# A fused graph layer and attention layer: several loads and vector instructions placed anew, and the last group of batches in another order

## The chip, the cores and the metric

The kernel runs on one core of a Trainium2 chip. The metric is the time on the device, in microseconds (us), from the first to the last instruction of the program and the little that lies around it; it is given as the median of several runs. The core has four compute engines with queues of their own: PE (TensorE, matrix products), DVE (VectorE), ACT (ScalarE) and POOL (GpSimd). SP (SyncE) only issues DMAs. Each engine works through its own list of instructions in order, and semaphores make an instruction wait for those of other engines that it depends on.

## The reference

The input is x of 64 batches of 256 rows of 512 numbers, and a symmetric 256 x 256 adjacency matrix of zeros and ones. Two layers follow each other, each with a residual and a norm:

```python
def _L0_gnn_ref(x, adj, W, b):
    Wi, Wj = (W[:, :Din], W[:, Din:])
    mi = einsum('bkd,od->bko', x, Wi)
    mj = einsum('bkd,od->bko', x, Wj)
    a = adj.astype(x.dtype)
    deg = a.sum(axis=1)
    return deg[None, :, None] * (mi + b) + einsum('ij,bjo->bio', a, mj)

def _L1_gnn_ref(h, adj, Wq, bq, Wk, bk, Wv, bv, Wo, bo):
    q, k, v = (split_heads(h @ W.T + c) for W, c in ((Wq, bq), (Wk, bk), (Wv, bv)))
    scores = einsum('bhqd,bhkd->bhqk', q, k) / 8
    scores = where(adj == 0, -inf, scores)
    out = einsum('bhqk,bhkd->bhqd', softmax(scores), v)
    return out.transpose(0, 2, 1, 3).reshape(b, n, 512) @ Wo.T + bo

x = _layernorm(x + _L0_gnn_ref(x, adj, L0_gnn_W, L0_gnn_b))
x = _layernorm(x + _L1_gnn_ref(x, adj, L1_gnn_Wq, ..., L1_gnn_bo))
```

There are 8 heads of 64 numbers. All is float32.

## The kernel before

**Groups and stages.** Batches are worked in 32 groups of two. The loop over g from 0 to 30 does the attention of group g and, woven into it, the graph layer (`Layer0`, objects `first` and `second`) of the two batches of group g + 1, called b1 and b2; b3 is the first batch of group g + 2. At the end of an iteration the v, q and k projections of group g + 1 are made. The last group, g = 31, has an end of its own after the loop. All groups are written out, with no loop on the chip.

**Products.** A product of float32 matrices is made from three products of rounded parts: each operand is cut into head, low and diff. `split_head` runs on ACT, `split_diff` on DVE, `split_low` on DVE or POOL as its last argument says. In PSUM one bank (`px`, or half of `pxy`) takes head times head and low times lift, another (`py`) takes diff times diff. The weights' parts (`factor`, 768 KB each) are read again from DRAM for each group into a ring of seven tiles: `bring` issues the load of the next one when one has been used up.

**PSUM banks.** There are three sorts: three single banks (`bank`), two tiles of two banks for scores (`score_banks`), and one for attention values (`value_bank`). The letter of a projection's step says from where its two banks come: "M" two single ones, "S" one pair of score banks, "A" one single one and the value bank.

**Attention.** Eight head pairs of a group, numbered w, each give: `scores(g, w)` (PE), of which the returned function adds the mask (DVE L910), takes the exponential (ACT L914) and adds the two halves of the keys (POOL L924); `values(g, w)` (PE); and after each second pair `divide_two`, which copies the values (ACT L958), forms the denominators on PE, takes their reciprocal (DVE L1009), moves it across partitions by two DMAs, and puts up a product for POOL that `multiply()` does (L952). The result, `aoT`, is cut into parts (`ao_parts`: batch i, chunks 0 and 1 are `upper`, 2 and 3 are `lower`; the head goes to a tile tagged qT, the diff to one tagged kT, the low part to one tagged v) and multiplied with the output weights in `o_steps`: `begin`, `go_on` and `own` for batch 0 of the group, `others` for batch 1. `adds(n)` (L830, L833) adds the product of row block n to the residual.

**The graph layer's result** of a row block goes through `add` (L613, neighbours' sum), `stat` (DVE L496 to L502, POOL L504) and `give` (ACT L509, L510), is sent to DRAM by `send_h`, fetched in another layout by `fetch_h`, and turned on DVE by `turn_h` (L517); then it is cut into the parts hA, hL and hD for the projections. x itself comes in twice: by `load_x` in rows (tile xh, of which there are five) and by `load_xB` for turning (`turn_x`); `x_head`, `x_low` and `x_diff` cut the turned x.

**Order.** Nearly every instruction goes through `in_order`, so each engine keeps the order in which the program calls it. Calls that follow each other in the program but belong to different engines have no order between them, apart from their dependencies. In the text, h11 and h10 are the row blocks 1 and 0 of b1; diff(upper), low(upper) and the like are the parts of `ao_parts(g, 1, ...)`, batch 1 of the group, unless batch 0 is named.

**The end.** `project(i, t, chunks)` multiplies `aoT` of row block t of batch i with the output weights in full float32, `finish` adds it, norms and stores. Before, the loop ran over the pairs w from 0 to 7, with the scores two pairs ahead:

```python
    last = NB * NC - 1
    for w in range(last + 1):
        values(g, w)
        multiply()
        if w == last - 1:
            project(0, 0, (0, 1, 2, 3))
            finish(0, 0)
        elif w % 2 and w < last:
            divide_two(g, w)
        if w + 2 <= last:
            scores(g, w + 2)()
```

Of the kernel before, what the change touches and what calls it, by code (L numbers as in the profile page):

```python
# [219 lines left out]
def unshifted_path(ctx, tc, flag, x, adj, wiT, wjT, b0, wqT, bq, wkT, bk, wvT, bv, woT, bo, out):  # L220
# [73 lines left out]
    def load_x(b):  # L294
        if b < B:
            xh[b] = p5.tile([P, NT, D], F32, tag="xh", name="xh")
            in_order(nc.sync.dma_start(out=xh[b], in_=x[b].rearrange("(t p) d -> p t d", p=P)))
# [738 lines left out]
    def projection_steps(g, kinds="", paired=True):  # L1036
        if paired:
            v = [v_pair(g, 0, "MS", False), v_pair(g, 1, "AS", True)]
        else:
            v = [v_step(g, i, t, kinds[NT * i + t], (i, t) == (NB - 1, 0)) for i in range(NB) for t in range(NT)]  # L1040
        q, k = ([qk_step(g, store, tag, bias, m, kinds[m]) for m in range(NC)]
                for store, tag, bias, kinds in ((qT, "qT", bq_sb, "SSSM"), (kT, "kT", bk_sb, "MMMA")))
        return v, q, k

    warm = value_bank("warm")
# [86 lines left out]
    for g in range(NG - 1):  # L1132
# [37 lines left out]
        if g:  # L1170
            for _ in range(NC):
                coming.pop(0)
                bring()

        values(g, 2)
        values(g, 3)
# [25 lines left out]

        values(g, 4)
        values(g, 5)
        load_x(b3)
        multiply()
        if g == 0:
            add_output_bias(0)
# [3 lines left out]
        now, later = scores(g, 6), scores(g, 7)  # L1212
        aoP[g] = three(("qT", "kT"))
        aoP[g].insert(1, None)
        now()
        split_head(*ao_parts(g, 0, lower))
        begin, go_on, own, adds, others = o_steps(g, early[0], lambda t: turn_h(b2, t))
        begin()
        later()
        second.neighbours()  # L1220
        values(g, 6)
        invert()
        fetch_h(b1, 1)
        values(g, 7)
        split_diff(*ao_parts(g, 0, lower))
        second.add(0)
        aoP[g][1], = three(("v",))
        first.give(0)
        multiply()
        second.add(1)  # L1230
        send_h(b1, 0)
        total_up = divide_two(g, 7)
        split_head(*ao_parts(g, 1, upper))
        fetch_h(b1, 0)
        go_on()
        split_low(*ao_parts(g, 0, lower), nc.gpsimd)
        own()
        h11 = turn_h(b1, 1)
        split_head(*h11)
        second.stat(1)  # L1240
        second.give(1)
        split_low(*ao_parts(g, 1, upper), nc.vector)
        split_diff(*ao_parts(g, 1, upper))
        multiply()
        split_head(*ao_parts(g, 1, lower))
        second.stat(0)
        adds(0)
        split_low(*ao_parts(g, 1, lower), nc.gpsimd)
        second.give(0)
        split_diff(*ao_parts(g, 1, lower))  # L1250
        h10 = turn_h(b1, 0)
        send_h(b2, 1)
        send_h(b2, 0)
        split_diff(*h11)
        split_head(*h10)
        adds(1)
        split_low(*h10, nc.vector)
        split_diff(*h10)
        total_up()
        fetch_h(b2, 1)  # L1260
        fetch_h(b2, 0)
        split_low(*h11, nc.gpsimd)
        first, second = Layer0(b3) if b3 < B else None, Layer0(b3 + 1)
        v, q_, k = projection_steps(g + 1)
        end = finish_steps(g)
        others()
        turn_x(b3)
        if g == 0:
            make_first("wj", 0)
            make_first("wj", 1)  # L1270
        v[0]()
        if g == 0:
            make_first("wj", 2)
            make_first("wj", 3)
            end_makes()
        x_head(b3)
        x_low(b3)
        v[1]()
        x_diff(b3)
        load_xB(b3 + 1)  # L1280
        run([end[0], q_[0], end[1], k[0], end[2], q_[1]])
        if first:
            first.graph_half(1, (0, 2, 1))
            first.take(1)
        run([end[3], k[1], end[4]])
        add_output_bias(b1)
        if g + 2 < NG:
            add_bias(b3)
        run([q_[2]])
        load_x(b3 + 1)  # L1290
        add_output_bias(b2)
        if first:
            first.cut_up(1)
        run([k[2], q_[3], end[5]])
        turn_x(b3 + 1)
        run([scores(g + 1, 0), scores(g + 1, 1)])
        if g + 2 == NG:
            k[3]()

    g = NG - 1
    wo_sb = p1.tile([P, NC, D], F32, tag="hA", name="wo_sb")
    load_wo(wo_sb, 0)
    outs = {}

    def project(i, t, chunks):
        if chunks[0] == 0:
            outs[i, t] = bank("po")
        for c in chunks:  # L1310
            matmul(outs[i, t], aoT[g][:, c, i * N + t * P:i * N + (t + 1) * P], wo_sb[:, c, :],
                   start=(c == 0), stop=(c == NC - 1))

    def finish(i, t):
# [4 lines left out]
        nc.sync.dma_start(out=out[b].rearrange("(t p) d -> p t d", p=P)[:, t, :], in_=r)  # L1319

    last = NB * NC - 1
    for w in range(last + 1):
        values(g, w)
        multiply()
        if w == last - 1:
            project(0, 0, (0, 1, 2, 3))
            finish(0, 0)
        elif w % 2 and w < last:
            divide_two(g, w)
        if w + 2 <= last:  # L1330
            scores(g, w + 2)()
    inverses = divide_at_once(g, last)
    project(0, 1, (0, 1, 2, 3))
    finish(0, 1)
    project(1, 0, (0, 1))
    project(1, 1, (0, 1))
    end_values(inverses)
    for t in range(NT):
        project(1, t, (2, 3))
        finish(1, t)  # L1340


# [49 lines left out]
```

## Time and profile before

| | us |
|---|---|
| median of 3 runs | 2952.39 (2951.73 to 2953.07) |
| the profiled execution | 2951.97 |
| its span, first to last instruction | 2950.1 |
| PE busy in the span | 2878.1 |
| DVE busy | 2265.1 |
| POOL busy | 1482.3 |
| ACT busy | 1309.4 |
| from one group's start to the next, steady groups | 90.1 to 91.6 |

The profile is of one execution. PE was granted 0.999 of its clock over the span. Times in views of the timeline are counted from the span's first instruction. In the table of waits, a line says which engine waited at which tile for whom, the total, how often, and the longest. In the timeline a line gives start, duration, engine, line of the kernel, operation, tiles (out<-in), and in brackets the idle time of the engine just before with what ended it. All matrix products stand at L286, since a helper issues them, so they are told apart by their tiles.

### The profile page before, as it was taken

To read this page: it belongs to the slowest core of one execution; us is meant where nothing else is said; L and a number is where in the kernel's file an instruction comes from. 1 tells how busy PE (TensorE), PEld (TensorE's weight loads), DVE (VectorE), ACT (ScalarE), POOL (GpSimd) and SP (SyncE) were. 2 spreads that over 40 slices of the span, in tenths; PEclk is the share of its full clock that TensorE was granted. 3 is DMA by queue.
4 is the path that set the end of the run, shared out by engine and by line. 5 is a ranking of instruction groups with operands and counts; after the bars stand their busy time and mean duration, and the time that the engine had idled before them with its cause. 6 is when DMAs were issued, how large, how long until landed. Compare 5 with 4: busy or idle time off the path is not lost.

```text
span 2950.1 us, 45509 instructions
## 1 busy us (share of the span) xinstructions
PE 2878.1 (98%) x16902; PEld 2140.1 (73%) x16902; DVE 2265.1 (77%) x3275; ACT 1309.4 (44%) x2412; POOL 1482.3 (50%) x1049
## 2 busy tenths in 40 slices
PE   9999999999999999999999999999999999999998
PEld 6577777777777777777777777777777777777775
DVE  5777787777877778877778777787777787777875
ACT  4444444444444444444444444444444444444443
POOL 3555555454555455454545544555545555454553
PEclk9999999999999999999999999999999999999999
DMA  7577766777666776667776677766677766777653
GB/s 251 194 258 239 247 218 218 255 245 266 217 219 239 266 247 230 212 226 264 242 247 222 221 249 252 268 212 215 238 267 240 246 214 215 257 248 261 213 211 116
DMA packets 303345, 690.54 MB, mean 234 GB/s; under 512 B 25744, under 2 KB 171280, under 8 KB 302864
## 3 DMA queue, kind: packets, MB, share of 16 engines
q1 hardware_dynamic: 282784, 588.02, 58.4%
q10 hardware_dynamic: 20336, 99.56, 9.5%
q8 instruction: 136, 2.23, 0.3%
q14 instruction: 89, 0.73, 0.1%
HBM read 589.04 MB, written 81.79 MB: 227 GB/s over the span
## 4 chain that ended last, share of the span: by engine, by line
PE 77%; DVE 15%; POOL 3%; DMA 3%; issue 1%; SPq 1%; ACT 1%; POOLq 0%; DVEq 0%; ACTq 0%
PE px L286 26%; PE pxy L286 20%; PE py L286 13%; PE ps L286 7%; PE pav L286 5%; PE pa L286 3%; DVE hF L517 2%; DMA hB<-h_cols 2%; DVE kT L683 2%; DVE spread L1009 2%; DVE st L496 2%; PE po L286 2%; DVE xh L833 1%; PE den L286 1%; DVE xh L830 1%
## 5 line engine op out<-in xcount | busy, mean ns | idle before, releaser
L924 POOL TENSOR_TENSOR pk<-pe 128x512 f32<-128x512 f32 x256 | 347.4, 1368 | 729.5 <-ACT pe L914 729.5
L914 ACT ACTIVATE pe<-pe 128x1024 f32<-128x1024 f32 x256 | 271.0, 1059 | 176.9 <-DVE pe L910 176.9
L504 POOL TENSOR_TENSOR rstd<-ve,mhalf 128x1 f32<-128x1 f32 x256 | 167.5, 654 | 343.4 <-DVE below L502 313.2
L910 DVE TENSOR_TENSOR pe<-ps,maskT 128x1024 f32<-128x1024 f32 x256 | 297.2, 1200 | 3.6 <-PE ps L286 3.6
L1009 DVE RECIPROCAL spread<-den 128x256 f32<-128x256 f32 x127 | 222.7, 1754 | 81.7 <-ACT aoT L958 51.8
L686 POOL TENSOR_TENSOR hL<-hF,hA 128x512 fp32r<-128x512 f32 x93 | 166.4, 1789 | 229.1 <-ACT hA L680 229.1
L774 DVE TENSOR_TENSOR kT<-py,kT 128x512 f32<-128x512 f32 x128 | 88.5, 692 | 226.2 <-ACT kT L773 226.2
L286 PE MATMUL ps<-qT,kT 64*128 64x256 f32 x2048 | 256.6, 390 | 0.0
L286 PE MATMUL pav<-pe,v_sb 128*32 128x256 f32 x4096 | 248.4, 382 | 3.5 <-DVE kT L774 1.5
L286 PEld LDWEIGHTS ps<-qT,kT 64*128 64x128 f32 x2048 | 187.3, 187 | 68.6 <-PE pav L286 26.3
L510 ACT ACTIVATE xh<-xh,shift,rstd 128x512 f32<-128x512 f32 x256 | 208.8, 816 | 8.6
L286 PEld LDWEIGHTS pav<-pe,v_sb 128*32 128x32 f32 x4096 | 120.0, 110 | 116.8 <-issue 24.4
L680 ACT ACTIVATE hA<-hF 128x512 fp32r<-128x512 f32 x124 | 78.3, 632 | 278.5 <-DVE hF L517 255.5
L286 PE MATMUL px<-factor,x_head 128*128 128x512 f32 x720 | 200.2, 400 | 0.0
L286 PE MATMUL py<-factor,x_diff 128*128 128x512 f32 x720 | 192.8, 390 | 2.0 <-ACT kT L773 2.0
L368 POOL TENSOR_TENSOR xh<-xh,degb 128x1024 f32<-128x1024 f32 x64 | 182.5, 2853 | 22.8 <-ACT degb L365 20.9
L286 PE MATMUL px<-factor,x_low 128*128 128x512 f32 x720 | 192.8, 390 | 0.0
L952 POOL TENSOR_TENSOR aoT<-aoT,spread 128x512 f32<-128x512 f32 x127 | 165.9, 1306 | 41.6 <-DMA spread<-spread 35.4
L686 POOL TENSOR_TENSOR x_low<-xT,x_head 128x1024 fp32r<-128x1024 f32 x60 | 144.2, 2403 | 67.6 <-ACT x_head L680 64.7
L286 PE MATMUL py<-hD,factor 128*128 128x512 f32 x640 | 175.9, 397 | 2.2 <-ACT kT L773 2.2
L286 PE MATMUL px<-hA,factor 128*128 128x512 f32 x640 | 175.7, 397 | 0.0
L496 DVE BATCH_NORM_STATS2 st<-xh 128x6 f32<-128x512 f32 x256 | 174.3, 681 | 0.2
(160 smaller groups left out, 6809.1 us busy)
## 6 DMA issues: line engine op xcount, KB each, us to landing
factor<-wi SPq DMA_DIRECT2D x120, 768.0 KB, 8.7
factor<-wo SPq DMA_DIRECT2D x120, 768.0 KB, 6.2
factor<-wv SPq DMA_DIRECT2D x93, 768.0 KB, 7.8
factor<-wk SPq DMA_DIRECT2D x93, 768.0 KB, 7.0
factor<-wq ACTq DMA_DIRECT2D x62, 768.0 KB, 7.6
factor<-wq SPq DMA_DIRECT2D x62, 768.0 KB, 7.4
xB<-in_x_dram SPq DMA_DIRECT2D x256, 128.0 KB, 4.1
xh<-in_x_dram SPq DMA_DIRECT2D x64, 512.0 KB, 3.9
```

What stands on the lines that cost most here:

```text
L286: in_order(nc.tensor.matmul(*args, **kw))
L368: in_order(nc.gpsimd.tensor_tensor(xh[b], xh[b], degb, ALU.add))
L496: order(nc.vector.bn_stats(st, t))
L504: order(nc.gpsimd.tensor_tensor(rstd, ve, mhalf, ALU.pow))
L510: order(nc.scalar.activation(t, t, AF.Identity, bias=shift, scale=rstd))
L686: in_order(engine.tensor_tensor(parts[1], src, parts[0].bitcast(F32), ALU.subtract))
L774: in_order(nc.vector.tensor_add(dst, Y, dst))
L910: in_order(nc.vector.tensor_add(pe.rearrange("p j t q -> p j (t q)"), ps.rearrange("p j t q -> p j (t q)"), maskT.rearrange("p t q -> p (t ...
L914: in_order(nc.scalar.activation(flat, flat, AF.Exp, scale=QSCALE, accum_out=etot[:, NB * g + i, pr:pr + 1]))
L924: in_order(nc.gpsimd.tensor_tensor(pk, pe[:, :, 0, :], pe[:, :, 1, :], ALU.add))
L952: in_order(nc.gpsimd.tensor_tensor(d, d, spread, ALU.mult))
L1009: in_order(nc.vector.reciprocal(rden, den))
```

## The change

It touches no formula and no tile of the steady loop; it moves calls, and rewrites the end.

- In the loop: `load_x(b3)` is called before pair 2's values, not after pair 5's. In the stretch from pair 6's scores to `others()`, the calls of ACT, DVE and POOL work are in another order, and `split_low` of h10 is POOL's, where it was DVE's. `load_xB(b3 + 1)` and `x_diff(b3)` come before `v[1]()`, where they came after. The finishing steps `end[...]`, the output biases and `load_x(b3 + 1)` stand elsewhere among the q and k projections.
- The last group: its projections q2, k2, q3 and k3 are no longer made in the iteration before but between the head pairs of the last group. The pairs go in the order 0, 1, 4, 5, 2, 3, 6, 7, so that the first four need only q0, k0, q1 and k1. `project` makes half of the chunks at a time, and three of these halves come between the pairs too. The output weights lie in two tiles of other tags. For this group, the banks of q2 and k3 are single ones ("SSMM", "MMMM").

```diff
--- before.py
+++ after.py
@@ -1039,7 +1039,9 @@
         else:
             v = [v_step(g, i, t, kinds[NT * i + t], (i, t) == (NB - 1, 0)) for i in range(NB) for t in range(NT)]
         q, k = ([qk_step(g, store, tag, bias, m, kinds[m]) for m in range(NC)]
-                for store, tag, bias, kinds in ((qT, "qT", bq_sb, "SSSM"), (kT, "kT", bk_sb, "MMMA")))
+                for store, tag, bias, kinds in (
+                    (qT, "qT", bq_sb, "SSSM" if g < NG - 1 else "SSMM"),
+                    (kT, "kT", bk_sb, "MMMA" if g < NG - 1 else "MMMM")))
         return v, q, k
 
     warm = value_bank("warm")
@@ -1171,6 +1173,7 @@
             for _ in range(NC):
                 coming.pop(0)
                 bring()
+        load_x(b3)
 
         values(g, 2)
         values(g, 3)
@@ -1202,7 +1205,6 @@
 
         values(g, 4)
         values(g, 5)
-        load_x(b3)
         multiply()
         if g == 0:
             add_output_bias(0)
@@ -1212,103 +1214,114 @@
         now, later = scores(g, 6), scores(g, 7)
         aoP[g] = three(("qT", "kT"))
         aoP[g].insert(1, None)
+        split_head(*ao_parts(g, 0, lower))
         now()
-        split_head(*ao_parts(g, 0, lower))
         begin, go_on, own, adds, others = o_steps(g, early[0], lambda t: turn_h(b2, t))
         begin()
         later()
         second.neighbours()
         values(g, 6)
         invert()
+        second.add(1)
+        first.give(0)
+        values(g, 7)
+        aoP[g][1], = three(("v",))
         fetch_h(b1, 1)
-        values(g, 7)
+        second.add(0)
+        send_h(b1, 0)
+        multiply()
         split_diff(*ao_parts(g, 0, lower))
-        second.add(0)
-        aoP[g][1], = three(("v",))
-        first.give(0)
-        multiply()
-        second.add(1)
-        send_h(b1, 0)
         total_up = divide_two(g, 7)
-        split_head(*ao_parts(g, 1, upper))
-        fetch_h(b1, 0)
         go_on()
         split_low(*ao_parts(g, 0, lower), nc.gpsimd)
         own()
         h11 = turn_h(b1, 1)
+        second.stat(1)
+        split_head(*ao_parts(g, 1, upper))
         split_head(*h11)
-        second.stat(1)
         second.give(1)
+        multiply()
         split_low(*ao_parts(g, 1, upper), nc.vector)
-        split_diff(*ao_parts(g, 1, upper))
-        multiply()
+        fetch_h(b1, 0)
         split_head(*ao_parts(g, 1, lower))
         second.stat(0)
+        split_diff(*ao_parts(g, 1, upper))
+        split_low(*ao_parts(g, 1, lower), nc.gpsimd)
         adds(0)
-        split_low(*ao_parts(g, 1, lower), nc.gpsimd)
         second.give(0)
         split_diff(*ao_parts(g, 1, lower))
+        send_h(b2, 1)
         h10 = turn_h(b1, 0)
-        send_h(b2, 1)
-        send_h(b2, 0)
         split_diff(*h11)
         split_head(*h10)
+        total_up()
         adds(1)
-        split_low(*h10, nc.vector)
         split_diff(*h10)
-        total_up()
+        send_h(b2, 0)
         fetch_h(b2, 1)
-        fetch_h(b2, 0)
         split_low(*h11, nc.gpsimd)
+        split_low(*h10, nc.gpsimd)
         first, second = Layer0(b3) if b3 < B else None, Layer0(b3 + 1)
         v, q_, k = projection_steps(g + 1)
-        end = finish_steps(g)
+        fetch_h(b2, 0)
         others()
         turn_x(b3)
         if g == 0:
             make_first("wj", 0)
             make_first("wj", 1)
         v[0]()
+        load_xB(b3 + 1)
         if g == 0:
             make_first("wj", 2)
             make_first("wj", 3)
             end_makes()
         x_head(b3)
+        x_diff(b3)
+        v[1]()
         x_low(b3)
-        v[1]()
-        x_diff(b3)
-        load_xB(b3 + 1)
-        run([end[0], q_[0], end[1], k[0], end[2], q_[1]])
+        end = finish_steps(g)
+        end[0]()
+        q_[0]()
+        end[1]()
+        k[0]()
+        q_[1]()
+        end[2]()
         if first:
             first.graph_half(1, (0, 2, 1))
             first.take(1)
-        run([end[3], k[1], end[4]])
-        add_output_bias(b1)
+        k[1]()
+        end[3]()
+        end[4]()
+        if g + 2 < NG:
+            q_[2]()
         if g + 2 < NG:
             add_bias(b3)
-        run([q_[2]])
+        if g + 2 < NG:
+            k[2]()
+        add_output_bias(b1)
         load_x(b3 + 1)
-        add_output_bias(b2)
         if first:
             first.cut_up(1)
-        run([k[2], q_[3], end[5]])
+        if g + 2 < NG:
+            q_[3]()
+        end[5]()
         turn_x(b3 + 1)
+        add_output_bias(b2)
         run([scores(g + 1, 0), scores(g + 1, 1)])
-        if g + 2 == NG:
-            k[3]()
 
 
 
     g = NG - 1
-    wo_sb = p1.tile([P, NC, D], F32, tag="hA", name="wo_sb")
-    load_wo(wo_sb, 0)
+    wo_sb = [p1.tile([P, 2, D], F32, tag=t, name="wo_sb") for t in ("xlow", "xdiff")]
+    for n, t in enumerate(wo_sb):
+        load_wo(t, 2 * n)
     outs = {}
 
-    def project(i, t, chunks):
-        if chunks[0] == 0:
-            outs[i, t] = bank("po")
-        for c in chunks:
-            matmul(outs[i, t], aoT[g][:, c, i * N + t * P:i * N + (t + 1) * P], wo_sb[:, c, :],
+    def project(i, t, half):
+        if half == 0:
+            outs[i, t] = score_bank("po") if i and t else bank("po")
+        for c in range(2 * half, 2 * half + 2):
+            matmul(outs[i, t], aoT[g][:, c, i * N + t * P:i * N + (t + 1) * P], wo_sb[half][:, c % 2, :],
                    start=(c == 0), stop=(c == NC - 1))
 
     def finish(i, t):
@@ -1319,24 +1332,31 @@
         nc.sync.dma_start(out=out[b].rearrange("(t p) d -> p t d", p=P)[:, t, :], in_=r)
 
     last = NB * NC - 1
-    for w in range(last + 1):
+    turns = (0, 1, 4, 5, 2, 3, 6, 7)
+    remaining = [q_[2], k[2], q_[3], k[3]]
+    for n, w in enumerate(turns):
+        if n < len(remaining):
+            remaining[n]()
         values(g, w)
         multiply()
-        if w == last - 1:
-            project(0, 0, (0, 1, 2, 3))
-            finish(0, 0)
-        elif w % 2 and w < last:
+        if n == 4:
+            project(0, 0, 0)
+        if n == 5:
+            project(0, 1, 0)
+        if n == 6:
+            project(1, 0, 0)
+        if n % 2 and w < last:
             divide_two(g, w)
-        if w + 2 <= last:
-            scores(g, w + 2)()
+        if n + 2 <= last:
+            scores(g, turns[n + 2])()
     inverses = divide_at_once(g, last)
-    project(0, 1, (0, 1, 2, 3))
-    finish(0, 1)
-    project(1, 0, (0, 1))
-    project(1, 1, (0, 1))
+    for t in range(NT):
+        project(0, t, 1)
+        finish(0, t)
+    project(1, 1, 0)
     end_values(inverses)
     for t in range(NT):
-        project(1, t, (2, 3))
+        project(1, t, 1)
         finish(1, t)
```

## The prediction

> **What bounds the kernel now.** I read the page first, then the waits of PE, then PE's busy time by stage, and last the timeline of one steady group and of the end.
>
> ```profile
> span 2950.1 us, 45509 instructions
> PE 2878.1 (98%) x16902; PEld 2140.1 (73%) x16902; DVE 2265.1 (77%) x3275; ACT 1309.4 (44%) x2412; POOL 1482.3 (50%) x1049
> ...
> PE py L286 <- DVE kT L683: 20.6, 32, 0.7
> PE px L286 <- POOL v L686: 19.9, 31, 2.0
> PE pxy L286 <- DVE xh L833: 7.2, 30, 0.3
> ```
>
> PE is busy 98%, and the change removes no matmul, so all it can win is PE's idle time: 2950.1 - 2878.1 = 72 us. Three waits of each group of two batches hold 47.7 us of it (columns: total us, times, longest us). All lie in one stage, the output product. This is the steady group at 1289 to 1379 us (start, duration, line, tiles, idle before):
>
> ```profile
> 1320.46 1.13 DVE L517 STREAM_TRANSPOSE hF<-hB 128x512 f32<-128x512 f32 x1
> 1321.49 0.65 DVE L496 BATCH_NORM_STATS2 st<-xh 128x6 f32<-128x512 f32 x1
> ...
> 1322.52 0.68 DVE L686 TENSOR_TENSOR v<-aoT,qT 128x512 fp32r<-128x512 f32 x1
> 1323.12 0.68 DVE L683 SCALAR_TENSOR_TENSOR kT<-qT,aoT 128x512 fp32r<-128x512 f32 x1
> 1323.72 0.69 DVE L496 BATCH_NORM_STATS2 st<-xh 128x6 f32<-128x512 f32 x1
> ...
> 1326.11 1.43 DVE L683 SCALAR_TENSOR_TENSOR kT<-qT,aoT 128x512 fp32r<-128x512 f32 x1
> ...
> 1323.58 1.37 POOL L952 TENSOR_TENSOR aoT<-aoT,spread 128x512 f32<-128x512 f32 x1
> ...
> 1325.70 1.29 POOL L686 TENSOR_TENSOR v<-aoT,qT 128x512 fp32r<-128x512 f32 x1 [0.23 <-ACT qT L680]
> ...
> 1321.41 0.73 PE L286 MATMUL px<-factor,v 128*128 128x512 f32 x2 [0.34 <-POOL v L686]
> 1327.59 0.50 PE L286 MATMUL py<-factor,kT 128*128 128x512 f32 x1 [0.72 <-DVE kT L683]
> 1330.63 0.50 PE L286 MATMUL pxy<-factor,hA 128*128 128x512 f32 x1 [0.24 <-DVE xh L833]
> ```
>
> See that DVE runs without a gap from the reciprocal of pair 7 (end 1320.40) to the last add of `adds(1)` (L833, end 1330.57): here PE waits for DVE's queue. The second `kT` lasts 1.43, not 0.68, because POOL is in L686 until 1326.99. The end of the program is the other loose stage:
>
> ```profile
> 2892.40:2907.30 14.90, 13.42 (x65) 10.14 (x63) 5.72 (x7) 5.94 (x10) 6.36 (x4) 1.00 0.30 88
> 2907.30:2931.00 23.70, 21.73 (x225) 10.76 (x226) 14.55 (x16) 9.84 (x21) 11.53 (x10) 1.00 0.19 40
> ```
>
> The columns are length, then PE, PEld, DVE, ACT, POOL. PE is idle 1.5 + 2.0 us in these rows, and its pair sums and values wait for exponentials.
>
> [...] The trace agrees: the 1.43 us above, with 0.55 us left after POOL's end. [...] Here a 128x512 matmul is drawn as 0.39 us but a new one starts every 0.23, so a printed wait hides some 0.16, and a restart costs 0.1 more; I count starts. [...] what follows on SP waits too; the trace shows it with `load_x` at 1363.68, ahead of a weight load that goes at 1364.16.
>
> **The change part by part.**
>
> *Steady groups, before the output product.* `split_head` of chunks 2, 3 goes ahead of pair 6's exponential: ACT has 0.63 more there (1313.15 to 1313.78), the exponential ends 0.4 later at 1314.8, and pair 7's still ends at 1315.95; the values of pair 6 start at 1316.2, so nothing. DVE now does the two neighbour adds (1.27) before `split_diff`; that ends at 1318.2, PE takes it at 1318.84, and the cover of 0.6 holds. POOL's pair sum is free of the port earlier, but the denominator is read at 1317.96 either way.
>
> *The POOL wait (0.34 here, up to 2.0)* stays: POOL's product waits for two spread DMAs, issued 1316.13 and 1316.65, landed 1318.05 and 1318.65, 1.9 and 2.0 us each, as long as spread DMAs with no x load about. The moved `load_x` landed at 1316.87, before them, so moving it wins nothing; at its new place (about 1298) it delays only the spread of pair 3, which lands at 1307.6 and is used at 1311.45.
>
> *DVE's order in the output product* is the core. New order after h11: stat(1), low(upper), stat(0), diff(upper), adds(0), diff(lower), h10, diff(h11), adds(1), diff(h10). stat(0) costs 1.07 (1323.80 to 1324.87). low(upper) ends 1323.20, so diff(upper) would begin at 1324.27; POOL's product L952, begun 1323.58, now runs 1.27 to 1324.85 and holds the port; then 0.58: 1325.43. PE wanted it at 1323.59 and had it at 1323.86; now it waits to 1325.48. From there 23 matmuls bring it to the v projection: 0.34 + 22 x 0.2295 = 5.39, so 1330.87, if diff(lower) is there in time (POOL's L686 to 1327.13, then 0.57 = 1327.70; PE asks at 1328.33: yes). adds(1): 1327.70 + 1.06 + 0.69 + 1.3 = 1330.75, also in time. Before, v began at 1330.63 and then stalled for diff(h10) at 1331.83; its matmul at 1332.40, less six of 0.229, gives an effective start of 1331.03. So -0.16 us a group: one long wait in place of three short ones. low(h10), 0.68 of DVE, goes to POOL, behind low(h11): 1329.5 to 1330.9, before PE's need at 1332.1. In the five groups with a POOL wait of 1.7 to 2.0, PE arrives late anyway, and the later diff(upper) costs about +0.3. Sum: 25 x -0.16 + 5 x 0.3 = -2.5 us.
>
> *After it.* `x_diff` before v's evictions: if POOL's `x_low` holds the port (2.4), the evictions end near 1346.4; the bank is wanted at 1347.6, and the next one, freed by ACT's k eviction at 1351.1, at 1352.1: covered by 1 us. In the first group these two waits are 0.50 and 2.04; the first grows by 0.75, the second goes, as `x_diff` then runs unblocked (1.2 for 1.89): -1. `load_xB` moves ahead of four weight loads on SP; its four issues take 2.6, so k1's weights issue at 1343 for 1340.29. They landed in 4 to 9 us and k1 is wanted at 1353.04: covered. `load_x(b3+1)` is passed by one weight load, which goes 2.8 earlier; no need is near. Output biases and `add_bias` change places on POOL, idle from 1360.9 to 1370.2: nothing.
>
> *The last group.* q2, k2, q3, k3 (2.72 each) go between the pairs, and three half products (1.83 each, from eight in 3.70) too. From k1's end at 2892.42: scores 0, 1 to 2894.4; four turns of projection 2.72, values 0.97, scores 0.98, with a denominator 0.55 each second turn, to 2914.1; two turns of values, half product, scores (one denominator) to 2922.15; values and a half product to 2924.95. Pair 7's exponential: reciprocal to 2922.95, add 1.2, exponential 1.1, so 2925.35, a wait of 0.4. Denominators to 2927.7, 0.3 for POOL's product, five half products of 1.83: 2937.2. Before, the last product ended at 2941.2, and 8.9 to the end are as before: -4.0. Exponentials have over 2 us of cover in the first turns. The last value bank is no longer taken by k3 (1.50 wait). The weights go to tiles free since 2863, so their twelve issues do not wait.
>
> Sum: -2.5 - 1.0 - 4.0 = -7.5. The profiled execution took 2951.97 (span 2950.1 and 1.9 around it), 0.4 below the median 2952.39, so 2944.9 in median terms.
>
> **Rivals.**
> 1. *The queue opens*: the port is not taken against diff(upper) and diff(lower). PE restarts at 1324.92, v begins at 1330.31, -0.72 in 25 groups and about -0.4 in five: -20 - 5 = 2927. For it: the order would then fit. Against: the 1.43 in every group.
> 2. *Gains cancel*: the steady stage ends a little late (+0.05 to +0.15 a group), the end wins 4 or less: about 2951. For it: 1330.75 and 1330.87 lie 0.1 apart, and many small edits hide.
> 3. *Slower*: diff(upper) loses the port twice. After POOL's product also rstd (0.55 to 0.99) slips in, so it ends at 1326.2; PE restarts at 1326.25, v at 1331.64, +0.61 a group: 30 x 0.61 - 5 = +13, 2965. It decides from an end of 1325.76 on, where 0.17 x 30 eats the 5 us. Against: after L686 at 1326.99 DVE got the port before POOL's next instruction, which lasted 1.75.
>
> **How the numbers follow.** Forecast 0.45 (own range 2941 to 2950), queue opens 0.17, cancel 0.24, slower 0.14. 0.2% (5.9 us) is about what can be told from no change: faster is below 2946.5. That is 0.36 of the forecast, all of the first rival, 0.03 of the second: 0.56; same 0.30; slower 0.14. The range 2927 to 2958 leaves half of the first rival and most of the third outside.
>
> **What would show it.** One wait of PE for `kT` near 1.7 us as printed in the steady groups, at chunk 0; no wait for `kT` at chunk 2 and none or little for `xh` L833; POOL's wait as before; diff(upper) near 1.15 us long. The last product ending some 44 us after k1's end (48.8 before). Wrong: a printed wait for `kT` of over 2 us, a PE wait for `factor`, or gaps between the last group's projections.

## The result and the profile after

The changed kernel took 2962.53 us (median of 8 runs, 2960.73 to 2969.67), the kernel before on the same chip 2953.43 (8 runs, 2951.73 to 2958.41). The ratio is 1.0032, 95% interval 1.0022 to 1.0041: slower by some 9 us, where 7.5 us of gain was forecast. The profiled execution took 2964.71 with a span of 2962.9.

The page of the changed kernel, and its table of PE's waits (total us, times, longest us):

```profile
span 2962.9 us, 45487 instructions
PE 2865.0 (97%) x16902; PEld 2143.7 (72%) x16902; DVE 2230.5 (75%) x3244; ACT 1308.5 (44%) x2412; POOL 1549.7 (52%) x1080
...
PE py L286 <- DVE kT L683: 46.9, 31, 1.9
PE px L286 <- POOL v L686: 18.6, 30, 2.0
PE px L286 <- POOL hL L686: 9.8, 22, 0.7
```

The long wait for `kT` is there as the prediction drew it, one of up to 1.9 us in each group; the wait for `xh` L833 has gone from the list, and POOL's `v` wait is as before. New is the third line: in 22 groups PE waits for the low part `hL`, at a place of which the prediction has no word. It lies 42 us after a group's start, counted here from ACT's instruction on `early`. The span divides as follows (worked out from the starts of these ACT instructions; us):

| kernel | to group 0 | group 0 | groups 1 to 29 | group 30 to the end |
|---|---|---|---|---|
| before | 114.3 | 96.0 | 2626.4 | 113.3 |
| after | 114.2 | 95.5 | 2640.1 | 113.1 |
| after, fetch ahead (below) | 114.6 | 94.5 | 2614.6 | 112.9 |
| before, low(h10) on POOL (below) | 114.9 | 95.4 | 2619.2 | 112.8 |

The loss between these two executions is in the steady groups: 13.7 us, of which the other stages win back 0.8. TensorE's clock has a part in it: it was granted at half for five stretches of 3.41 us in the profile after and for one before, each some 1.7 us (last section). One of the steady groups in the changed kernel, starting at 1209.5 (timeline: start, duration, engine, line, tiles, idle before):

```profile
1236.37 1.20 DVE L683 SCALAR_TENSOR_TENSOR kT<-qT,aoT 128x512 fp32r<-128x512 f32 x1
1236.98 1.00 POOL L504 TENSOR_TENSOR rstd<-ve,mhalf 128x1 f32<-128x1 f32 x1
1237.62 0.50 PE L286 MATMUL py<-factor,kT 128*128 128x512 f32 x1 [1.70 <-DVE kT L683]
...
1241.02 0.32 ACTq L456 DMA_DIRECT2D factor<-wv  x1
1241.51 0.34 ACTq L456 DMA_DIRECT2D factor<-wq  x1
...
1248.83 1.12 DVE L517 STREAM_TRANSPOSE hF<-hB 128x512 f32<-128x512 f32 x1 [1.04 <-DMA hB<-h_cols]
1250.69 1.80 POOL L686 TENSOR_TENSOR hL<-hF,hA 128x512 fp32r<-128x512 f32 x1 [3.68 <-ACT hA L680]
1252.54 0.50 PE L286 MATMUL px<-factor,hL 128*128 128x512 f32 x1 [0.65 <-POOL hL L686]
```

and the fetches of h in it (all of tile hB in the window 1236 to 1256; the last start is the fetch of block 0 of b2, called the fetch here):

```profile
L707 SPq DMA_DIRECT2D hB<-h_cols x2: 333/355/377, 1239.7 to 1241.6; - x2
DMA to landing us min/median/max: 2.7/4.9/7.1
```

The same in the kernel before, in the group that starts at 1297.3 (timeline and tile hB):

```profile
1322.62 0.99 POOL L504 TENSOR_TENSOR rstd<-ve,mhalf 128x1 f32<-128x1 f32 x1 [1.27 <-DMA spread<-spread]
1324.91 0.55 POOL L504 TENSOR_TENSOR rstd<-ve,mhalf 128x1 f32<-128x1 f32 x1
1329.21 0.37 ACTq L456 DMA_DIRECT2D factor<-wq  x1
1336.04 1.11 DVE L517 STREAM_TRANSPOSE hF<-hB 128x512 f32<-128x512 f32 x1
1337.89 1.81 POOL L686 TENSOR_TENSOR hL<-hF,hA 128x512 fp32r<-128x512 f32 x1 [2.54 <-ACT hA L680]
1339.75 0.19 PEld L286 LDWEIGHTS px<-factor,hL 128*128 128x128 f32 x1 [0.32 <-POOL hL L686]
```

```profile
L707 SPq DMA_DIRECT2D hB<-h_cols x2: 333/358/383, 1327.2 to 1329.1; - x2
DMA to landing us min/median/max: 2.8/3.7/4.6
```

Read it as a chain. Diff(upper), late, runs from 1236.37 to 1237.57, and the `rstd` of stat(0), begun within it at 1236.98, lasts 1.00 for 0.55: it ends 0.41 after diff(upper). Diff(upper) itself was begun within POOL's product L952 (1235.76 to 1237.02) and lasts 1.20 for 0.68, to 0.55 after that one's end. "The port" in the recorded texts stands for such a lengthening of one of two overlapping instructions of DVE and POOL; only the overlaps measured here are meant. (The first of the six lines of before is the `rstd` of stat(1), which the kernel before already paid in this way: 0.99 beside low(upper), DVE's from 1322.52 to 1323.20.) With it `give(0)`, `send_h` and the fetch come 0.3 to 0.4 later. Before, the fetch went at 1329.1, just ahead of ACT's load of wq (768 KB) at 1329.21, and landed in 4.6 us. Now it goes at 1241.6, just behind that load at 1241.51, and takes 7.1. DVE comes to the transpose and waits 1.04; the head, then POOL's low part, follow. And `hL` had no room: before, it ended at 1339.70 and PE's weight load took it at 1339.75. Over groups 1 to 29 the fetch lands at a median of 36.8 us into the group before and 39.0 after; DVE waits over 0.3 us for it in none of them before and in 25 after. The changed kernel holds its own comparison: in these 25 groups the fetch is issued behind the load of wq and takes 6.4 to 8.0 us, in the other four it is ahead and takes 4.9 to 5.6.

### The profile page after: what moved, and what is told of

The parts are those of the page before. It is cut to its first block, busy times and chain, and to the rows that moved or that the text cites. A ratio compares the mean times of both kernels' runs of the same rounds, so it can differ in the third digit from the quotient of the medians.

```text
span 2962.9 us, 45487 instructions
## 1 busy us (share of the span) xinstructions
PE 2865.0 (97%) x16902; PEld 2143.7 (72%) x16902; DVE 2230.5 (75%) x3244; ACT 1308.5 (44%) x2412; POOL 1549.7 (52%) x1080
## 4 chain that ended last, share of the span: by engine, by line
PE 72%; DVE 14%; POOL 5%; issue 4%; DMA 3%; ACT 1%; SPq 1%; DVEq 0%; POOLq 0%; ACTq 0%
PE px L286 25%; PE pxy L286 16%; PE py L286 12%; PE ps L286 7%; PE pav L286 6%; DVE hF L517 3%; PE pa L286 3%; POOL hL L686 3%; DMA hB<-h_cols 2%; PE po L286 2%; DVE spread L1009 2%; DVE kT L683 2%; DVE st L496 2%; PE den L286 1%; DVE xh L830 1%
## 5 line engine op out<-in xcount | busy, mean ns | idle before, releaser
L924 POOL TENSOR_TENSOR pk<-pe 128x512 f32<-128x512 f32 x256 | 334.9, 1324 | 683.2 <-ACT pe L914 673.8
L504 POOL TENSOR_TENSOR rstd<-ve,mhalf 128x1 f32<-128x1 f32 x256 | 181.4, 709 | 362.7 <-DVE below L502 335.3
L686 POOL TENSOR_TENSOR hL<-hF,hA 128x512 fp32r<-128x512 f32 x124 | 205.9, 1661 | 196.0 <-ACT hA L680 188.4
L686 POOL TENSOR_TENSOR x_low<-xT,x_head 128x1024 fp32r<-128x1024 f32 x60 | 175.2, 2920 | 66.8 <-ACT x_head L680 63.8
L952 POOL TENSOR_TENSOR aoT<-aoT,spread 128x512 f32<-128x512 f32 x127 | 162.6, 1280 | 54.2 <-DMA spread<-spread 41.5
```

The source lines that it names most:

```text
L504: order(nc.gpsimd.tensor_tensor(rstd, ve, mhalf, ALU.pow))
L686: in_order(engine.tensor_tensor(parts[1], src, parts[0].bitcast(F32), ALU.subtract))
L924: in_order(nc.gpsimd.tensor_tensor(pk, pe[:, :, 0, :], pe[:, :, 1, :], ALU.add))
L952: in_order(nc.gpsimd.tensor_tensor(d, d, spread, ALU.mult))
```

## The experiments

Each has 5 to 21 runs; the kernel before, in the same sessions, had medians of 2952.8 to 2954.3. Three theories stood at the start: that the fetch falls behind a weight load; that a wait of over 1.7 us costs PE some of its clock (five stretches of 3.41 us at half clock in the profile after, one before); and that POOL, with low(h10) added, is late with `hL`.

**1. Diff(upper) back ahead of stat(0), all else as changed.**

```diff
         split_low(*ao_parts(g, 1, upper), nc.vector)
+        split_diff(*ao_parts(g, 1, upper))
         fetch_h(b1, 0)
...
         second.stat(0)
-        split_diff(*ao_parts(g, 1, upper))
```

> The kernel after, with one edit undone: diff(upper) stands ahead of stat(0) again. Three theories of the loss of 9 to 13 us. Clock theory: the one long wait of PE (1.7 us as printed) makes the granted clock drop to half for 3.4 us in some groups (five times in the profile of after, once in that of before, 1.7 us each). Fetch theory: rstd of stat(0) now meets diff(upper) at the port, takes 1.00 for 0.55, so the send and the fetch of h of the second batch are 0.3 later and the fetch falls behind a 768 KB weight load (landing 39.2 us into the group for 36.4), which gives the new wait for hL. POOL theory: the wait for hL comes from low(h10), which is POOL's now. Clock and fetch theory: with the edit undone both losses go, 2950 to 2954, granted clock 0.998 to 0.999, no wait for hL. POOL theory: the wait for hL of some 0.4 stays in most groups, 2957 to 2960.

2941.55 us, ratio to before 0.9959 (0.9945 to 0.9972): 21 us off the changed kernel, and below both. PE's waits in it:

```profile
PE py L286 <- DVE kT L683: 20.4, 35, 0.7
PE px L286 <- POOL v L686: 19.2, 31, 2.2
PE pxy L286 <- DVE xh L833: 7.1, 30, 0.2
...
PE px L286 <- POOL hL L686: 2.9, 6, 0.6
```

Low(h10) is still POOL's, and the wait for `hL` is nearly gone: the POOL theory falls. The other two remain. Neither gave a time under the kernel before, so the change also wins something; experiment 6 finds it.

**2. The long wait filled.** The changed kernel, with four more copies of the first matmul of `others()` ahead of it. The first matmul proper starts the sum anew, so the output stays the same.

```diff
             banks.update({2: pair("A"), 3: pair("S")})
+            for _ in range(4):
+                matmul(banks[2][0], aoP[g][0][:, 0, 2 * P:3 * P], coming[0][:, 0, :], start=True, stop=False,
+                       skip_group_check=True)
```

> The kernel after, with four more runs of the first matmul of the product of batch 1, just ahead of the long wait (the same operands into the same bank, which the real one starts anew, so nothing else is computed): 0.92 us of PE work in place of idle time, the wait for kT as printed some 0.8 for 1.7. No dependency and no other engine changes. Clock theory: the half-clock stretches go (clock 0.998 or more in all runs), and the time falls by 5 to 7 us, to 2955 to 2958, less what the filler costs in the groups where PE comes late anyway (under 1 us in all). If the wait itself is the loss and the clock only goes along with it: 2961 to 2964, no change. The wait for hL stays in either case.

2964.28 us, 1.0031 (1.0019 to 1.0044), no different from the changed kernel; `kT` waits 22.5 us in all for 46.9, `hL` 10.0 in 20, four stretches at half clock. Half of the long wait filled won nothing, so the idle time itself is not what makes the loss. The clock theory is not settled by it: three of the four stretches stand behind waits for POOL's `v` of 1.8 to 2.2 us, which the filler leaves as they are, and the clock of its six runs, 0.996 to 0.997, lies between that of the changed kernel and that of the kernel before (last section).

**3. The fetch ahead of the weight load.** The changed kernel, with wq's load issued by SP, where it stands behind the fetch; diff(upper) stays late.

```diff
                 if c == 1:
-                    bring(issuer=nc.scalar)
+                    bring()
                     h1 = turn(1)
```

> The kernel after, with the second weight load of the product of batch 1 issued from SP in place of ACT, so that it stands behind the fetch of h in SP's own order. Fetch theory: h of the second batch lands at about 36.4 us into the group again, the wait for hL (9.8 us printed in 22 groups, some 15 with what the printed wait hides) goes, 2948 to 2955, unless the time comes back as a longer wait elsewhere. POOL theory: the wait for hL stays, 2960 to 2964. The wait for kT and the half-clock stretches stay in both.

2938.5 us, 0.9955 (0.9942 to 0.9969): 24 us off the changed kernel. Its waits, and tile hB in the group from 1292.0 (window 1318 to 1336):

```profile
PE py L286 <- DVE kT L683: 45.3, 31, 1.9
PE px L286 <- POOL v L686: 21.0, 31, 2.2
```

```profile
L707 SPq DMA_DIRECT2D hB<-h_cols x2: 332/355/378, 1322.3 to 1324.2; - x2
DMA to landing us min/median/max: 2.8/3.8/4.9
```

The long wait for `kT` is all there; the one for `hL` does not occur at all. The fetch goes as late as in the changed kernel (median 32.15 us into the group, 32.21 there, 31.84 before), but with wq behind it lands at 37.3, for 39.0; wq's weights land at 39.3 in both. Not the 0.3 us, but the order in which the two transfers go, is what costs. The time is under what either theory gave, for the reason of experiment 6; and some 5 of the 24 us go with the clock (an estimate, last section).

**4. The new last group alone**, in the kernel before (the diff of the end as in the change).

> The kernel before, with the new last group alone. The prediction's sum: 4 us faster than before, 2949 to 2950. By the trace of after: the last group from the first early part to the end takes 113.1 us for 113.3, so nothing, 2952.5 to 2954.

2954.26 us, 1.0001 (0.9993 to 1.001, 13 runs): the rewritten end is worth nothing.

**5. Diff(upper) behind stat(0), alone in the kernel before.** The edit of experiment 1 the other way round.

> The kernel before with one edit: diff(upper) stands behind stat(0), as in the changed kernel; low(h10) stays on DVE, all else is as before. Fetch theory: this one edit makes rstd of stat(0) collide with diff(upper) at the port (1.00 us for 0.55), sends the fetch of (b2, 0) behind ACT's second weight load, and so carries the whole loss: the waits for kT as in the changed kernel (45 to 47 us in 31 waits), waits for hL in 20 or more groups, and since low(h10) still delays DVE none of the gain: 2965 to 2975. Rival, the loss needs several of the moved calls together (the sends and fetches also stand elsewhere in the program): no wait for hL, 2950 to 2958.

2962.39 us, 1.0035 (1.0021 to 1.0048).

```profile
PE py L286 <- DVE kT L683: 45.2, 31, 2.3
PE px L286 <- POOL v L686: 21.7, 31, 2.1
...
PE px L286 <- POOL hL L686: 2.8, 8, 0.6
```

One edit is enough to lose what the whole change lost, though less than expected (2.0 of it in group 0), and with few printed waits for `hL`. Its trace is 9.9 us longer than that of the kernel before and has four stretches at half clock for one, so some 5 us of this are the clock's. The rest is the chain: the fetch goes at 32.24 and lands at 39.07, as in the changed kernel, but DVE, which still has low(h10) here, does not reach the transpose before 39.09 (38.81 in the kernel before). PE's matmul on `hL` then comes 0.36 later than before (medians 42.88 and 42.52), below what is printed as a wait in most groups.

**6. Low(h10) on POOL, alone in the kernel before.**

```diff
-        split_low(*h10, nc.vector)
...
         split_low(*h11, nc.gpsimd)
+        split_low(*h10, nc.gpsimd)
```

> The kernel before with one edit: low(h10) is POOL's, behind low(h11), where it was DVE's. The changed kernel with diff(upper) back and the one with the fetch ahead of the weight load both gain about 0.4 us a group on the kernel before, in the v projection and in the products of the second batch. Theory A, the gain comes from DVE being free of low(h10) by 0.68 us: 30 x 0.3 to 0.45 = 9 to 13 us, so 2941 to 2945, with the three waits of the output product as before. Theory B, the gain comes from the other moves (x_diff, load_x, load_xB, the adds): 2951 to 2957.

2941.72 us, 0.9964 (0.995 to 0.9978): theory A. This one move makes 11 of the 16 us by which experiment 3 beats the kernel before. All other edits together are left with 5, less than one of these intervals is wide (8 us).

**7. Wq's load on SP, alone in the kernel before** (the edit of experiment 3).

> The kernel before with one edit: the second weight load of the output product's second part is issued by SP, behind the fetch of (b2, 0), where ACT issued it. In the kernel before the fetch is already ahead of this load (31.81 and 31.91 us into the group). Fetch theory: nothing to win, 2951 to 2957. Rival, the gain of the same edit in the changed kernel came from the weights' later start or from ACT being free of the issue, whatever the fetch does: 2935 to 2945.

2952.42 us, 1.0 (0.9992 to 1.0009). Where the fetch is ahead of the load anyway, the issuer is worth nothing.

**8. Diff(lower) put between the two adds of adds(0), and another end**, on the changed kernel with the edits of 1 and 3.

```diff
+        adds(0, lambda: split_diff(*ao_parts(g, 1, lower)))
         split_low(*ao_parts(g, 1, lower), nc.gpsimd)
-        adds(0)
         second.give(0)
-        split_diff(*ao_parts(g, 1, lower))
...
```

> The changed kernel with diff(upper) ahead of stat(0) again, the second weight load on SP, diff(lower) between the two instructions of adds(0), and at the end q2 ahead of the last group's first scores and batch 0's first row block finished before pair 7's denominators. In the traces DVE starts 0.03 us after ACT's split_head ends and POOL 0.08 after it, so diff(lower) should get the port ahead of POOL's low part: 0.57 to 0.7 us long for 1.42, no wait for kT at chunk 2 (0.7 a group before), none or little for xh. Theory: up to 0.5 us a group in the steady stage on 2940, and 1 to 2 us at the end: 2922 to 2930. Rival, POOL's low part then ends 0.5 us later and PE waits for it instead (a wait for v or hL of 0.3 or more): 2936 to 2942.

2937.07 us, 0.9946 (0.9932 to 0.9959): the time of the rival, but by another wait than it named. Its waits, and four lines of its timeline in the group from 1289.1:

```profile
PE pxy L286 <- DVE xh L833: 30.3, 30, 1.6
PE px L286 <- POOL v L686: 19.4, 30, 2.3
PE py L286 <- DVE kT L683: 2.5, 11, 0.5
```

```profile
1317.52 0.69 DVE L683 SCALAR_TENSOR_TENSOR kT<-qT,aoT 128x512 fp32r<-128x512 f32 x1 [0.18 <-ACT qT L680]
1317.57 1.81 POOL L686 TENSOR_TENSOR v<-aoT,qT 128x512 fp32r<-128x512 f32 x1 [0.23 <-ACT qT L680]
1319.33 2.98 POOL L686 TENSOR_TENSOR hL<-hF,hA 128x512 fp32r<-128x512 f32 x2
1319.75 1.43 DVE L683 SCALAR_TENSOR_TENSOR hD<-hA,hF 128x512 fp32r<-128x512 f32 x1
```

Diff(lower) started 0.05 us before POOL's low(lower) and lasted 0.69 (POOL's 1.81, for a median of 1.29 in the kernel before), the wait for `kT` at chunk 2 is gone, but diff(h11), begun within POOL's low(h11), lasted 1.43, so adds(1) ended where it had, and PE waited 1.0 for it in each group. The end got longer, 115.6 for 112.9: the half product that was moved ahead of pair 7's denominators waited 1.5 for POOL's `aoT`, and where it had stood PE now waited 1.4 for DVE's.

**9. The fetch put last by hand**: experiment 6, with wq's load and then the fetch on SP.

> The kernel before with low(h10) on POOL (2941.7 us by itself), and now the fetch of (b2, 0) put by hand behind the second weight load of the output product's second part, both on SP; diff(upper) stays ahead of stat(0), so no collision with rstd and no long wait for kT. Fetch theory: the order of these two transfers alone makes the loss of the changed kernel: h of (b2, 0) lands near 39 us into the group, as in the changed kernel, for 37.6, POOL's hL ends 0.8 later, PE waits for it in 20 or more groups, and the time goes up by 15 to 25 us, to 2957 to 2967. Rival, the loss comes from the long wait in place of three short ones (a restart of PE, or its clock), and the fetch only adds to it: at most half of that, 2942 to 2950, with hL waits or none.

2961.37 us, 1.0031 (1.0019 to 1.0043): the time that the fetch theory gave, but not by the way it gave. SP found a free tile and issued wq's load before ACT's of wv; PE then waited for wv's weights, and not for `hL`:

```profile
PE pxy L286 <- DMA factor<-wv: 13.2, 14, 1.5
```

The profile is of the fastest of six runs (2956.64). The experiment shows that the order of these transfers can be worth some 20 us, not which of them is the one.

**10. The fetch behind both loads, on ACT**: experiment 6, with the fetch issued by ACT after wv's and wq's loads.

```diff
                     bring(issuer=nc.scalar)
+                    then()
                     h1 = turn(1)
...
-        fetch_h(b2, 0)
-        others()
+        others(lambda: fetch_h(b2, 0, nc.scalar))
```

> The kernel before with low(h10) on POOL (2941.7 us by itself), and the fetch of (b2, 0) issued by ACT right behind its two weight loads, so that the order is first weight load, second weight load, fetch; no weight load is issued earlier than before and diff(upper) stays ahead of stat(0). The run with the fetch put last on SP had also brought the second weight load ahead of the first, and PE waited for the first; this one leaves that out. Fetch theory: h of (b2, 0) lands near 39 us into the group for 37, POOL's hL ends some 0.6 to 1.0 later than 42.2, PE waits for hL in 20 or more groups and for weights no more than before: 2955 to 2970. Rival, what cost 19.7 us in that run was the weights alone, and hL has room: 2940 to 2946.

2955.97 us, 1.0012 (1.0005 to 1.0018, 21 runs), so 13 us more than experiment 6, each against its own runs of before (the profiled execution is the fastest of the 21, 2952.75). Its waits, and tile hB (window 1326 to 1345):

```profile
PE py L286 <- DVE kT L683: 19.6, 32, 0.7
PE px L286 <- POOL hL L686: 7.4, 14, 0.7
```

```profile
L707 ACTq DMA_DIRECT2D hB<-h_cols x1: 366/366/366, 1329.6 to 1329.6; - x1
DMA to landing us min/median/max: 2.8/5.0/7.1
```

The transfer takes 7.1 us again in this group, lands at a median of 38.9 for 37.6 in experiment 6, and PE waits for `hL`, with no late diff(upper), no long wait for `kT`, and a clock as in the kernel before (0.996 to 0.999). Of the 1.3 us of delay 0.7 is the later issue (32.57 for 31.86), so this is not the order alone. It reached the lower end of what was expected, with 14 waits for the 20.

**11. Adds(1) ahead of diff(h11)**: the steady loop of experiment 8, the changed kernel's end.

```diff
         h10 = turn_h(b1, 0)
+        adds(1)
         split_diff(*h11)
         split_head(*h10)
         total_up()
-        adds(1)
```

> The changed kernel with diff(upper) ahead of stat(0) again, the second weight load on SP, diff(lower) between the two instructions of adds(0), and adds(1) ahead of diff(h11); the end is the changed kernel's. In the run with diff(lower) moved, the chunk-2 wait went but diff(h11) then lost the port to POOL's low(h11) (1.43 us for 0.69), so adds(1) ended where it had, and PE waited 1.0 for it. Theory, the stage from the reciprocal to the v projection is bound by what DVE and POOL need of the port together, so this order only moves the wait on to diff(h11) or low(h10): 2934 to 2941. Rival, adds(1) was last by its place alone: v starts up to 0.9 us earlier and stays ahead: 2915 to 2928.

2929.68 us, 0.9924 (0.991 to 0.9937), the fastest here and below both kernels. It lies between the two expectations: the v projection starts 1.2 us earlier than in experiment 8 (32.26 for 33.45, medians), then waits up to 0.7 for diff(h11) (29 waits, 19.1 us in all); behind it a quarter is kept (0.31 at the low part of h10, 34.40 for 34.71; the steady groups are 0.26 shorter).

**12. Q2 ahead of the last group's first scores**, on experiment 11.

> The run with adds(1) earlier (2929.7), and in the last group q2 stands ahead of the first scores, so that k1's eviction on DVE is done before pair 1's scores ask for it. Theory: PE's wait of 0.60 for k1's kT goes and nothing takes its place: from the last group's start to the end 112.2 for 112.8, 2929.1, which the median can't tell from 2929.7. Rival: q2 is then missing as cover further on and the values wait for an exponential or for aoT (the run with the other end had 0.55 there): 112.8 or more.

2931.99 us (2930.23 to 2933.43), not to be told from experiment 11. In the trace the last stretch is 112.24 for 112.78: the 0.60 wait for k1 has gone, and a 0.55 wait for ACT's `aoT` has come further on. The net of 0.54 in one execution each is as the theory had it, but this is too small to count as shown.

## Why the prediction was wrong, point by point

*The bound, and the stages ahead of the output product: right.* No new wait of PE stands before the output product, and POOL's wait is 18.6 us in all for 19.9.

*The core: the walk on DVE and PE was right, but its gain is not the wait's.* Diff(upper) lasts 1.20 ("near 1.15"), the printed wait at chunk 0 is 1.3 to 1.9 (0.6 to 0.7 in the five groups where PE waits long for POOL), the waits at chunk 2 and for `xh` are gone. At the low part of h10 in the v projection the changed kernel is 0.23 us earlier than the kernel before (34.71 us into the group for 34.94, medians), for the -0.16 worked out. But the two edits in that sum come apart in experiments 5 and 6: with diff(upper) late and nothing else this matmul comes at 35.03, 0.09 later than before, and with low(h10) on POOL and nothing else at 34.70. "One long wait in place of three short ones" won nothing; the gain is low(h10)'s.

*The step that failed is "Sum: 25 x -0.16 + 5 x 0.3 = -2.5 us".* The walk followed the late diff(upper) into PE and stopped at the v projection's second row block. It didn't follow it into the instruction that overlaps it on POOL. That is `rstd`, 1.00 for 0.55, and give, send and fetch hang from it; the prediction prices stat(0) for what it makes diff(upper) wait, and not for what diff(upper) makes it wait. Nor does it follow the fetch, whose order against ACT's weight loads was decided by 0.1 us before, nor say that POOL's `hL` of the last row block was taken by PE 0.05 us after it was ready. The sum also counts every matmul at full clock, where the runs had a mean of 0.9952, for 0.9980 before. Experiments 1 and 5 show that late diff(upper) makes the loss, experiment 3 and the changed kernel's own groups that the order of the fetch does, and experiment 10 that a late fetch costs without the rest. The missing term is 24 us (changed kernel against experiment 3): some 19 for the fetch behind the load and some 5 for the clock, as an estimate. The kernel before showed the size of the first link, 0.99 for the `rstd` of stat(1). And hardly any of the signs that the prediction named for being wrong occurred, since they watch the stages that it had walked.

*The same step has a second miss, of the other sign.* Low(h10) off DVE was given its effect on diff(h10) and no more. Everything behind it on DVE moves up too: the transpose of the last row block comes at 38.30 in experiment 3 for 38.81, so `hL`, without slack, ends 0.5 earlier. Experiment 6 measures the move at 11 us. So the steady groups would have won 11.9 in the trace of experiment 3, not 2.5, had the fetch stayed ahead.

*"The first group: -1"*: 0.5 after, and 1.5 with the fetch ahead. The size is right within what a single execution shows.

*"The last group: -4.0" failed in its terms.* By stretches (length, then PE, PEld, DVE, ACT, POOL busy, clock, DMA), from k1's end to the last product and from there to the end, after and then before:

```profile
2905.51:2952.58 47.07, 46.04 (x313) 24.59 (x312) 27.70 (x39) 18.84 (x36) 20.27 (x17) 1.00 0.16 46
2952.58:2962.90 10.32, 0.38 (x2) 0.30 (x2) 2.71 (x12) 3.83 (x8) 1.48 (x3) 0.75 0.30 107
```

```profile
2892.42:2941.20 48.78, 45.33 (x315) 25.43 (x313) 27.85 (x37) 18.59 (x37) 18.75 (x15) 1.00 0.21 57
2941.20:2950.10 8.90, 0.12 (x3) 0.03 (x1) 2.22 (x10) 2.21 (x4) 1.09 (x2) 0.72 0.19 65
```

The first stretch was to take 44.8. A projection between other work takes 2.94 from its first matmul to the next work's, for the 2.72 that the sum took from a row of projections (4 x 0.22); eight scores take 1.06 for 0.98; three half products 1.91 for 1.83; and pair 1's scores wait 0.60 for k1's eviction, which the old order had hidden behind q2. That is 2.4, less 0.2 for the exponential of pair 7, whose wait was 0.19 for 0.4; 2.3 is what the stretch is over. The second stretch was taken over as 8.9 from the old order; but there one row block was finished long before, and now four are finished together: the last store takes 3.9 us to land for 2.65, and the small instructions on `rhi` and `good` stand within the last norm on DVE. Why the store takes longer is not shown. All this gives back 1.4 of the 1.7.

*The rivals.* The result lies near "slower" (2965) by accident, since that mechanism did not occur: `rstd` did not slip in ahead of diff(upper), it came behind it and paid. "Gains cancel" is true of the end alone.

*That DVE's and POOL's instructions lengthen each other* held where they overlap: `rstd` lasts 1.00 for 0.55 and diff(upper) 1.20 for 0.68 in the changed kernel, diff(h11) 1.43 for some 0.7 in experiment 8. The prediction applied it to one of the two instructions that meet.

## What to carry to other kernels

When an instruction is moved so that it overlaps one of another engine that was seen to lengthen it or be lengthened by it (here diff(upper) 1.20 for 0.68, `rstd` 1.00 for 0.55), price both, and follow the one that is delayed through its DMAs to whoever reads what they bring. Where two queues issue transfers within some tenths of a microsecond of each other, their order is part of the kernel, here some 19 us of it (the estimate above; a landing after 7.1 us for 4.6): before moving anything ahead of it, list issue and landing times side by side, and put the small transfer that is needed first ahead by construction, not by chance. Work taken off a busy engine is worth what all the instructions behind it gain, down to the last one that has no slack. Don't count several short waits of TensorE drawn together into one long one as the same idle time: here the runs with the long one had mean clocks of 0.9952 to 0.9970, and all but one of the other experiments 0.9975 to 0.9984.

## What was not expected of the hardware

A 256 KB fetch issued 0.1 us behind a 768 KB load instead of 0.1 ahead of it took 7.1 us for 4.6 to land, though the load was issued by another engine's queue. Over groups 1 to 29 the medians are 6.8 (changed kernel, behind in 25) and 5.0 (kernel before, ahead in 28). In experiment 3, where a load of this size follows it by 0.4, it took 4.9. Being ahead by 0.1 is no guarantee: in the kernel before these 28 took 4.4 to 7.0, and in experiments 1 and 6 the median is 5.9 and 5.4, up to 7.8; but in no trace did a fetch behind the load take less than 5.6. Why the order of issue on two queues weighs so much is not shown.

TensorE's clock is granted at half in single stretches of 3.41 us inside the steady groups, five in the profile after and one before; around one of them in the changed kernel (length, busy times as above, PEclk, DMA share):

```profile
2785.10:2787.10 2.00, 0.63 (x3) 0.54 (x4) 1.97 (x5) 1.58 (x3) 2.00 (x3) 1.00 0.17 49
2787.10:2790.50 3.40, 3.40 (x10) 2.65 (x9) 3.40 (x5) 1.64 (x4) 2.74 (x3) 0.50 0.61 164
2790.50:2793.90 3.40, 3.40 (x16) 2.77 (x15) 3.25 (x5) 0.82 (x3) 1.24 (x1) 1.00 0.84 281
```

Ten matmuls touch the half-clock stretch where sixteen touch the next, so a stretch costs some 1.7 us. Four of the five stand just behind a wait of PE of 1.8 to 1.9 us, here one of 1.80 for `kT` that ended at 2786.47, the fifth behind three short ones (0.42, 0.23 and 0.64); the one in the kernel before stands behind a wait of 2.04 for POOL's `v`. But between 100 and 2900 us PE of the changed kernel has sixteen waits of 1.7 us or more, twelve of them with no such stretch behind, and experiment 3, with the same long waits, has one stretch only. What decides whether a wait is followed by one is not shown.

How much of the 9 us is the clock's can be estimated from the clock of the runs. The changed kernel's eight runs had 0.993 to 0.996 (mean 0.9952), the 70 of the kernel before in the experiments' sessions 0.996 to 0.999 (mean 0.9980). Over 2960 us this is a difference of some 8 us, as an estimate: nearly all of the 9. The fetch's 19 or so are set off by what the other edits win, low(h10) above all. Against experiment 3, whose five runs had a mean of 0.9970, it is some 5 us, since diff(upper) is late there too. The other three with diff(upper) late had means of 0.9966 to 0.9970 (experiments 2, 3 and 5), those with it early 0.9975 to 0.9984, but for experiment 12 with 0.9970. In experiment 3 alone, two of five runs had 0.995 and took 2944 and 2945 us, the other three 0.998 to 0.999 and 2935 to 2939. No experiment here moves the clock and leaves all else, so this part is worked out and not shown by an edit.
